# Four convolution layers on one core: smaller input batches in layer 0, and layer 1's chunks placed among layer 2's

## The chip, the core and the metric

The kernel runs on one core of a Trainium2 chip. The time is the device time of one execution in microseconds; before the change it is 16901.53 us, the median of three runs (16893.86 to 16957.51). The profile is one execution of 16909.8 us. PE is the tensor engine, PEld its weight loads, DVE the vector engine, ACT the scalar engine, POOL is GpSimd and SP the sync engine, of which the last two only issue transfers here.

## The reference

x is a batch of 32 images of 8 channels and 256 x 256 pixels. Four layers follow one another, each of the form x + f(gn(x)), where gn normalises each of four groups of two channels of an image:

```python
x = x + L0(gn(x))   # cellular automaton, learned automaton and a gate between them
x = x + L1(gn(x))   # 3x3 convolution of values quantised to -127..127, one scale for all images
x = x + L2(gn(x))   # 3x3 convolution
x = x + L3(gn(x))   # 5x5 mean of each channel
```

Layer 0 computes, from its normalised input (called drive where it is the automaton's):

```python
grid = drive
for _ in range(15):
    mapped = 3.9 * grid * (1 - grid)
    local = conv3x3(mapped, K_local, one kernel per channel)
    grid = 0.85 * (0.7 * mapped + 0.3 * local) + 0.15 * drive
cml = clip(grid, 0.0001, 0.9999)
nca = sigmoid(conv1x1(relu(conv3x3(x, Wp, bp)), Wu, bu))     # 8 -> 128 -> 8 channels
g = sigmoid(conv1x1(relu(conv3x3([x, cml, nca], Wg1, bg1)), Wg2, bg2))
out = g * cml + (1 - g) * nca
```

Because layer 1's scale needs the largest value of all 32 normalised images, layer 0 has to end for all images before layer 1 begins. So the kernel has two stages.

## The kernel before

**Stage one, layer 0.** Two streams of work are interleaved by hand; the order in which the program issues instructions is the order of each engine. The first stream is `lattice(b)`, the 15 steps of the automaton of image b. Each step has two halves of three channels: products with the neighbourhood (L391 from `state`, L393 from `rings`, the edge values that SyncE's transfers bring together), an addition on VectorE (L402), a square on ScalarE (L419) and the next transfer of `rings` (L259). Two more channels are done on VectorE alone, by nine taps a step (L338). The second stream is `gated()`, which computes the learned automaton and the gate of image b-1. After every piece, `lattice` says how many microseconds of other work should follow it, and the main loop takes that much from `gated()`. `errands` and `store` issue the transfers that bring images in and put the normalised ones into DRAM (`xn_d` with a border, `nr_d`, `xr_d`, `cr_d`), one at each half step.

`gated()` walks over n, a pair of row indices in each of the 16 blocks of an image; an image has 8 such n, and there are 256 in all. The input of the 3x3 convolution lies in tiles `im`: 24 x 3 partitions hold 8 channels at three horizontal and three vertical offsets, so that one product of 72 rows (L633) makes 512 pixels of 128 hidden channels. ScalarE takes each product through relu into `hh` (L638). A batch is four such products; during the next batch `second()` multiplies the four by `wu_sb` (L609), and when an n is complete `close` applies the sigmoid into `nh` (L587) and issues the edges `above` and `below` of it for the gate (L480). After each batch `pieces` runs the next piece of every gate that is due: first its loads `xq`, `cq`, edges and `xc` (L516, L480, L521), two batches later three products with `xq`, then with `cq`, then with `nh` (L530), then the edges (L538), the second convolution (L547), and at last the blend on VectorE and the store to `x1_d` (L560 to L568).

The `im` tiles are filled by `load(n, half)`: six transfers on GpSimd's queue (L504), one for each vertical offset and row index, each of 24 rows of 8248 bytes, for half of an n, which are 8 products. There are two buffers. When the eight products of one half are issued, the loads of the same half of n+1 are put among the first four products of the following half.

**Stage two, layers 1 to 3.** Three images are under way at once. A turn b of the loop (L864) issues layer 3 of image b-3, then layer 2 of image b-1, then layer 1 of image b. `among(work, tasks)` issues one piece of a layer's products and then the small tasks that are hung on that piece. Layers 1 and 2 have eight chunks of 512 columns; a chunk is four products (L726 three times, L730 once for the rows beside the block) in a PSUM tile of a pool of five. Layer 2's chunk is float32 and is taken out by VectorE (L771), layer 1's is bf16 and is taken out by ScalarE (L755) and added to by VectorE (L756); both then have their statistics counted (L772, L757). Layer 3 has four groups of ten products (L812 and L825), taken out by L832.

The rows beside a block come by `beside` (L143) on SyncE's queue: `xb` from `xh`, `qb` from `qh`, two transfers each. Statistics are computed by `stats_parts` in small steps, which go back and forth between VectorE, TensorE (L104, L111) and ScalarE, and by `by_group`, which brings the four groups' values to all partitions (L131 on VectorE, L133 on TensorE). In the code before, layer 1's statistics and its normalisation for layer 2 (`normal2`, L761), and the quantisation of the next image (`quantize1`, L742 to L706), are hung on layer 3's pieces. Layer 3's normalisation (`normal3`, L793) is hung on layer 2's chunks, and the statistics of layer 2's output are hung on layer 1's chunks. Layer 2's output goes to DRAM (L777) and comes back in another layout (`load3`, L786).

Of the kernel before, what the change touches and what calls it, by code (L numbers as in the profile page):

```python
# [9 lines left out]
F32 = mybir.dt.float32  # L10
# [7 lines left out]
P = 128  # L18
# [3 lines left out]
RB = H // HB  # L22
# [44 lines left out]
def kernel(  # L67
# [70 lines left out]
    def beside(queue, t, src, q):  # L138


        row, long = HB * WP, (HB - 1) * WP - 2
        for i, (p, to, at) in enumerate(((P - C, 1, 0), (0, 0, 1))):
            queue.dma_start(  # L143
                t[q + 24 * i : q + 24 * i + 24, :, :].rearrange("p k w -> p (k w)")[
                    :, to * WP : to * WP + long
                ],
                window(src, p * row + at * WP, [[row, C], [1, 3], [1, long]]),
            )
# [18 lines left out]

    with ExitStack() as es:
        wt = es.enter_context(tc.tile_pool(name="wt0", bufs=1))
        imp = es.enter_context(tc.tile_pool(name="im", bufs=2))  # L170
        qp = es.enter_context(tc.tile_pool(name="quarters", bufs=2))
        hp = es.enter_context(tc.tile_pool(name="h", bufs=3))
        ps_c = es.enter_context(tc.tile_pool(name="ps_c", bufs=3, space=PSUM))
# [313 lines left out]
        def gated():  # L487
# [1 line left out]

            run = 8 * WP - 2
            SLOTS = [k % 8 for k in range(HB)]
            due = {}
            ims, sums, halos = [], {}, {}

            def load(n, half):
                b, r2 = divmod(n, NCH)
                im = imp.tile([72, 2, 8 * WP], F32, name="im")
                ims.append(im)  # L500
                for dy in range(3):
                    for k in range(2):
                        at = ((2 * r2 + k) * RB + 8 * half + dy) * WP
                        nc.gpsimd.dma_start(  # L504
                            im[24 * dy : 24 * dy + 24, k, 0:run],
                            window(xn_d[b % 3], at, [[HP * WP, C], [1, 3], [1, run]]),
                        )
                        yield
# [87 lines left out]
            def pieces(batch):  # L596
                for g in due.pop(batch, ()):
                    w = next(g, None)
                    if w is not None:
                        due.setdefault(batch + 1, []).append(g)  # L600
                        yield w
# [3 lines left out]
            def second():  # L605
                n, pn, four = late.pop()
                for hh, r in four:
                    i, q = divmod(r, 4)
                    nc.tensor.matmul(  # L609
                        pn[32 * q : 32 * q + 32, :], wu_sb[:, i, :], hh,  # L610
                        start=i == 0, stop=i == 3,
                    )
                if four[-1][1] == RB - 1:
                    close(n, pn)

            batch, quarter = 0, None
            for half in range(2):
                for _ in load(0, half):
                    pass
            coming = iter(())  # L620
            for n in range(B * NCH):
                place[0] = n
                if n % 2 == 0:
                    quarter = {}

                due.setdefault(batch + 5, []).append(gate(n, quarter))
                for half in range(2):
                    im = ims.pop(0)
                    for rows in ((0, 1, 2, 3), (4, 5, 6, 7)):
                        four = []  # L630
                        for i, j in enumerate(rows):
                            ph = psum.tile([P, 512], F32, name="ph", tag="ps")
                            nc.tensor.matmul(  # L633
                                ph.rearrange("p (k w) -> p k w", w=W), wp_sb,
                                im[:, :, j * WP : j * WP + W], start=True, stop=True,
                            )
                            hh = hp.tile([P, 512], F32, name="hh", bufs=6)
                            nc.scalar.activation(hh, ph, AF.Relu, bias=bp_sb)  # L638
                            four.append((hh, 8 * half + j))
                            next(coming, None)  # L640
                            if i % 2 == 0:
                                next(coming, None)
                            if i == 1 and late:
                                second()
                                yield 1.05
                            yield 0.87
                        if half == 0 and rows[0] == 0:
                            pn = ps_n.tile([P, 512], F32, name="pn")
                        late.append((n, pn, four))
                        yield from pieces(batch)  # L650
                        batch += 1
                    coming = load(n + 1, half) if n + 1 < B * NCH else iter(())
            second()
            yield 1.05
            while due:
# [24 lines left out]
    with ExitStack() as es:  # L680
# [59 lines left out]
        def quantize1(b, x1, k):  # L740
            t = two.tile([P, 1024], F32, name="tq")
            nc.vector.tensor_scalar(  # L742
                t, x1[:, bass.ts(k, 1024)], stat1[:, b, 0:1], stat1[:, b, 1:2],
                ALU.subtract, ALU.mult,
            )
            quantize(
                qh[:, 4 * k : 4 * k + 4, 1 : 1 + W],
                t.rearrange("p (r w) -> p r w", w=W), sc[:, 0:1],
            )
# [17 lines left out]
        def layer2(b, x2, bn):  # L767
            for i in range(NCH):
                ps = conv3(xh, xb2, w2_sb, i)
                c = x2[:, bass.ts(i, 512)]  # L770
                nc.vector.scalar_tensor_tensor(c, ps, b2_sb, c, ALU.add, ALU.add)  # L771
                nc.vector.bn_stats(bn[:, i, :], c)  # L772
                yield
            x3 = x3_d[b % 2]
            for r in range(RB):
                m = r % 4 * 4 + r // 4
                nc.gpsimd.dma_start(  # L777
                    window(x3, r * W, [[H * W, C], [RB * W, HB], [1, W]]),
                    x2[C * m : C * m + C, :].rearrange("p (k w) -> p k w", w=W),
                )  # L780
# [64 lines left out]
        def among(work, tasks):  # L845
            for i in range(8):
                next(work, None)
                for task in tasks.get(i, ()):
                    task()
            for _ in work:  # L850
                pass
# [4 lines left out]
        def begin(bn):  # L856
            st = small.tile([P, 2], F32, name="st")
            parts = stats_parts(psum, bn, st, gavr_sb, "ps")
            next(parts)
            return st, parts  # L860

        with tc.manual_schedule():
            x1s[0] = load1(0)
            for b in range(B + 3):  # L864
                if b + 1 < B:
                    x1s[b + 1] = load1(b + 1)
                tasks = {i: [] for i in range(8)}
                if 1 <= b <= B:
                    st, parts = sums.pop(1)
                    for i in range(4):  # L870
                        tasks[i].append(step(parts))
                    tasks[3].append(lambda: normal2(x2s[b - 1], st))
                if b < B:
                    for k, i in enumerate((0, 1, 2, 4)):
                        tasks[i].append(lambda k=k: quantize1(b, x1s[b], k))
                    tasks[5].append(lambda: beside(nc.sync, qb, qh, 0))
                among(layer3(b - 3, ys.pop(b - 3)) if b >= 3 else iter(()), tasks)
                tasks = {}
                if 2 <= b <= B + 1:
                    for g in range(4):  # L880
                        tasks[g] = [lambda g=g: normal3(ys[b - 2], gss[b - 2], g)]
                    tasks[3].append(beside3)
                bn2 = small.tile([P, NCH, 6], F32, name="bn")
                among(layer2(b - 1, x2s[b - 1], bn2) if 1 <= b <= B else iter(()), tasks)
                tasks = {}
                if 1 <= b <= B:
                    st3, parts3 = begin(bn2)
                    for i in range(4):
                        tasks[i + 1] = [step(parts3)]

                    def groups():
                        gss[b - 1] = by_group(psum, st3)

                    tasks[6] = [groups]
                    ys[b - 1] = load3(b - 1)
                bn1 = small.tile([P, NCH, 6], F32, name="bn")
                if b < B:
                    x2s[b] = two.tile([P, NPX], F32, name="x2")
                among(layer1(b, x1s[b], x2s[b], bn1) if b < B else iter(()), tasks)
                if b < B:  # L900
                    sums[1] = begin(bn1)


def laid_out(inputs):
# [133 lines left out]
```

## Time and profile before

| stretch | from, us | to, us | what runs |
|---|---|---|---|
| first automaton | 0 | 387 | `lattice` of image 0 alone |
| stage one | 387 | 13768 | `lattice` of image b with `gated` of image b-1 |
| last gate | 13768 | 14025 | `gated` of image 31 alone |
| stage two | 14025 | 16910 | layers 1 to 3 in turns of 85.4 us |

The borders are the first and last starts of L633 and L393. Engines over the whole span: PE 15762.1 us busy, DVE 11707.7, ACT 5744.5, POOL 3820.6. The largest groups are L338 on DVE (3840 instructions of 1284 ns) and L633 on PE (8192 records, 4218.6 us busy; a float32 product stands as two records). L504 on POOL has 3072 instructions of 565 ns mean, 193.3 KB each, with a median of 9.0 us from issue to landing. In a line of the profile's waits, the first part is who waited, the second for whom, then the total, the number of waits and the longest. In a timeline line, the two numbers are start and duration, and the bracket has the idle time ahead of it and what ended it. In a line of stretches there follow, after the busy times and counts of the five engines in the order PE, PEld, DVE, ACT, POOL, the granted clock of TensorE, the share of DMA time and GB/s.

### The profile page before, as it was taken

The numbers are of one execution on the slowest core, as the hardware profiler recorded it, in microseconds if no ns is written. First come the engines' busy times: TensorE is split into PE (matmuls) and PEld (weight loads), VectorE is DVE, ScalarE is ACT, GpSimd is POOL, SyncE is SP. The second block draws the span as 40 slices with busy tenths as digits, with TensorE's granted clock in tenths as the row PEclk, the third lists the DMA queues.
The fourth block names the chain that finished last, engine by engine and source line by source line (L and its number), as shares of the span: only waits on it lengthen the run. The fifth ranks groups of instructions, "written<-read, shape, count | busy, mean of one in ns | idle before, by whom it ended". The sixth has DMA issues, their size and how long they took to land. (4 is left out here: it accounts for less than half of the span.)

```text
span 16909.8 us, 135970 instructions
## 1 busy us (share of the span) xinstructions
PE 15762.1 (93%) x42888; PEld 6291.4 (37%) x42888; DVE 11707.7 (69%) x14652; ACT 5744.5 (34%) x8862; POOL 3820.6 (23%) x6419
## 2 busy tenths in 40 slices
PE   5999999999999999999999999999999997999999
PEld 2333333333333333333333333333333332333333
DVE  7777777777777777777777777777777754555554
ACT  2333333333333333333333333333333342111110
POOL 1222222222222222222222222222222222111111
PEclk7999999999999999999999999999999998999999
DMA  4766666666677667676666666666666664555554
GB/s 102 148 140 140 137 145 139 140 140 139 143 144 144 143 142 144 144 145 137 141 143 145 140 140 144 139 137 140 142 145 141 142 125 103 113 111 111 114 114 97
DMA packets 861099, 2275.88 MB, mean 135 GB/s; under 512 B 296860, under 2 KB 500628, under 8 KB 780388
## 3 DMA queue, kind: packets, MB, share of 16 engines
q0 software_dynamic: 507904, 1492.90, 41.6%
q1 hardware_dynamic: 352484, 774.29, 23.0%
q8 instruction: 350, 5.73, 0.2%
q14 instruction: 361, 2.96, 0.1%
HBM read 1078.63 MB, written 471.38 MB: 92 GB/s over the span
## 5 line engine op out<-in xcount | busy, mean ns | idle before, releaser
L338 DVE SCALAR_TENSOR_TENSOR acc<-strip,taps_sb,acc 128x1024 f32<-128x1024 f32 x3840 | 4930.3, 1284 | 122.4 <-DMA strip<-strip 2.4
L633 PE MATMUL ph<-im,wp_sb 72*128 72x512 f32 x8192 | 4218.6, 632 | 492.8 <-ACT hh L638 248.2
L638 ACT ACTIVATE hh<-ph,bp_sb 128x512 f32<-128x512 f32 x4096 | 2764.0, 691 | 4873.6 <-PE ph L633 4818.6
L402 DVE SCALAR_TENSOR_TENSOR psc<-psc,flat 128x512 f32<-128x512 f32 x2880 | 1935.6, 696 | 3256.2 <-PE psc L393 3236.6
L391 PE MATMUL psc<-state,patch_sb 128*128 128x512 f32 x5760 | 2844.8, 632 | 74.5 <-ACT state L419 63.7
L393 PE MATMUL psc<-rings,ring_sb 80*128 80x512 f32 x5760 | 2727.2, 610 | 176.4 <-DMA rings<-state 176.0
L504 POOL DMA_DIRECT2D im<-xn_d x3072 | 1721.9, 565 | 3909.3 <-PE ph L633 3394.7
L633 PEld LDWEIGHTS ph<-im,wp_sb 72*128 72x128 f32 x8192 | 1522.0, 197 | 2694.9 <-issue 1887.0
L419 ACT ACTIVATE state<-psc,minus 128x512 f32<-128x512 f32 x2688 | 1690.9, 691 | 1816.3 <-DVE psc L402 1750.7
L391 PEld LDWEIGHTS psc<-state,patch_sb 128*128 128x128 f32 x5760 | 1131.5, 202 | 1730.3 <-issue 1411.0
L393 PEld LDWEIGHTS psc<-rings,ring_sb 80*128 80x128 f32 x5760 | 1112.4, 194 | 1636.6 <-issue 1592.5
L812 PE MATMUL psv<-xr,w_sb 128*128 128x512 f32 x2560 | 1200.6, 619 | 1.3 <-DVE xr L793 1.3
L609 PE MATMUL pn<-hh,wu_sb 128*32 128x512 f32 x8192 | 1172.8, 629 | 2.4 <-ACT hh L638 2.3
L568 POOL DMA_DIRECT2D x_d<-xc x256 | 149.9, 586 | 3896.8 <-DVE xc L563 3670.5
L777 POOL DMA_DIRECT2D x_d<-x x512 | 304.2, 610 | 2115.5 <-DVE x L771 1854.0
L530 PE MATMUL pg<-xq,wg_sb 128*128 128x512 f32 x1536 | 759.0, 633 | 0.0
L755 ACT ACTIVATE x<-psv,b_sb,sc 128x512 f32<-128x512 f32 x256 | 199.8, 780 | 1598.2 <-PE psv L730 1592.7
L812 PEld LDWEIGHTS psv<-xr,w_sb 128*128 128x128 f32 x2560 | 489.9, 197 | 660.4 <-issue 656.2
L726 PE MATMUL psv<-xh,w_sb 128*128 128x512 f32 x1536 | 708.0, 597 | 19.4 <-DVE xh L761 9.8
L530 PE MATMUL pg<-cq,wg_sb 128*128 128x512 f32 x1536 | 717.6, 603 | 0.0
L480 POOL DMA_DIRECT2D below<-nh x288 | 197.3, 685 | 1860.5 <-ACT nh L587 1860.5
L338 DVE SCALAR_TENSOR_TENSOR acc<-strip,taps_sb,d 128x1024 f32<-128x1024 f32 x480 | 613.0, 1277 | 0.0
(163 smaller groups left out, 12238.2 us busy)
## 6 DMA issues: line engine op xcount, KB each, us to landing
im<-xn_d POOLq DMA_DIRECT2D x3072, 193.3 KB, 9.0
rings<-state SPq DMA_DIRECT2D x1920, 159.5 KB
rings<-state SPq DMA_DIRECT2D x1920, 106.3 KB
strip<-strip SPq DMA_DIRECT2D x960, 126.0 KB
xn_d<-xb POOLq DMA_DIRECT2D x128, 516.0 KB, 11.9
nr_d<-xb POOLq DMA_DIRECT2D x128, 516.0 KB, 10.0
xq<-nr_d POOLq DMA_DIRECT2D x128, 516.0 KB, 5.2
cq<-cr_d POOLq DMA_DIRECT2D x128, 516.0 KB, 7.7
```

Source lines behind the costliest of these rows:

```text
L338: nc.vector.scalar_tensor_tensor(acc, strip[:, dy : dy + RQ, dx : dx + W], taps_sb[:, 3 * dy + dx : 3 * dy + dx + 1], d2 if dy == 1 and dx ...
L391: nc.tensor.matmul(pss[-1], patch_sb[:, c, :], inner(c), start=True, stop=False)
L393: nc.tensor.matmul(pss[c % HALF], ring_sb[:, c, :], rings[half][:, c % HALF, 0 : TX * SY].rearrange("p (x y) -> p x y", y=SY)[:, :, 0:TY], ...
L402: nc.vector.scalar_tensor_tensor(ps, ps, FLOOR, dr[:, c], ALU.max, ALU.add)
L419: nc.scalar.activation(inner(c), pss[c % HALF], AF.Square, bias=minus)
L504: nc.gpsimd.dma_start(im[24 * dy : 24 * dy + 24, k, 0:run], window(xn_d[b % 3], at, [[HP * WP, C], [1, 3], [1, run]]),)
L530: nc.tensor.matmul(o, wg1_sb[:, s, dx, :], src[:, :, dx : dx + W], start=s == dx == 0, stop=False,)
L609: nc.tensor.matmul(pn[32 * q : 32 * q + 32, :], wu_sb[:, i, :], hh, start=i == 0, stop=i == 3,)
L633: nc.tensor.matmul(ph.rearrange("p (k w) -> p k w", w=W), wp_sb, im[:, :, j * WP : j * WP + W], start=True, stop=True,)
L638: nc.scalar.activation(hh, ph, AF.Relu, bias=bp_sb)
L726: nc.tensor.matmul(o, w[:, dx, :], src[:, 2 * i : 2 * i + 2, dx : dx + W], start=dx == 0, stop=False,)
L812: nc.tensor.matmul(pss[k].rearrange("p (c w) -> p c w", w=W), w3_sb[:, dx, :], xr[:, k, mine, dx : dx + W], start=dx == 0, stop=stop,)
```

## The change

Two parts, independent of each other.

In `gated()`, `load(n, four)` now fills a tile for four products, a quarter of an n, and there are four buffers. A load again has six transfers, of half the bytes. They are issued among the first two products of the batch that follows, for the same quarter of n+1. The point is that data be asked for three batches ahead of its use. The order of the products and of everything else in the stream stays.

In stage two, layer 1 of image b and layer 2 of image b-1 are issued together, a chunk of layer 2 and then one of layer 1, so that VectorE has a longer stretch of TensorE work to keep up with. Layer 3's statistics can't be hung on layer 1 any longer; they move to layer 3's pieces of the next turn, next to those of layer 1's output. The fourth quantisation and the transfer of `qb` move up by one piece.

```diff
-        imp = es.enter_context(tc.tile_pool(name="im", bufs=2))
+        imp = es.enter_context(tc.tile_pool(name="im", bufs=4))
...
-            run = 8 * WP - 2
+            run = 4 * WP - 2
...
-            def load(n, half):
+            def load(n, four):
+
                 b, r2 = divmod(n, NCH)
-                im = imp.tile([72, 2, 8 * WP], F32, name="im")
+                im = imp.tile([72, 2, 4 * WP], F32, name="im")
                 ims.append(im)
                 for dy in range(3):
                     for k in range(2):
-                        at = ((2 * r2 + k) * RB + 8 * half + dy) * WP
+                        at = ((2 * r2 + k) * RB + 4 * four + dy) * WP
...
-                for half in range(2):
+                for i in range(4):
                     im = ims.pop(0)
-                    for rows in ((0, 1, 2, 3), (4, 5, 6, 7)):
-                        four = []
-                        for i, j in enumerate(rows):
...
-                            next(coming, None)
-                            if i % 2 == 0:
-                                next(coming, None)
-                            if i == 1 and late:
-                                second()
-                                yield 1.05
-                            yield 0.87
...
+                    four = []
+                    for j in range(4):
...
+                        for _ in range(3):
                             next(coming, None)
+                        if j == 1 and late:
+                            second()
+                            yield 1.05
+                        yield 0.87
...
-                    coming = load(n + 1, half) if n + 1 < B * NCH else iter(())
+                    coming = load(n + 1, i) if n + 1 < B * NCH else iter(())
...
                 tasks = {i: [] for i in range(8)}
+                if 2 <= b <= B + 1:
+                    st3, parts3 = sums.pop(2)
+                    for i in range(4):
+                        tasks[i].append(step(parts3))
+
+                    def groups():
+                        gss[b - 2] = by_group(psum, st3)
+
+                    tasks[5].append(groups)
...
-                    for k, i in enumerate((0, 1, 2, 4)):
-                        tasks[i].append(lambda k=k: quantize1(b, x1s[b], k))
-                    tasks[5].append(lambda: beside(nc.sync, qb, qh, 0))
+                    for k in range(4):
+                        tasks[k].append(lambda k=k: quantize1(b, x1s[b], k))
+                    tasks[4].append(lambda: beside(nc.sync, qb, qh, 0))
...
-                among(layer2(b - 1, x2s[b - 1], bn2) if 1 <= b <= B else iter(()), tasks)
...
+                ones_ = layer1(b, x1s[b], x2s[b], bns[0]) if b < B else iter(())
+
+                def both():
+                    for _ in layer2(b - 1, x2s[b - 1], bns[1]) if 1 <= b <= B else range(8):
+                        next(ones_, None)
+                        yield
+
+                among(both(), tasks)
+                if 1 <= b <= B:
+                    sums[2] = begin(bns[1])
+                    ys[b - 1] = load3(b - 1)
                 if b < B:
-                    sums[1] = begin(bn1)
+                    sums[1] = begin(bns[0])
```

More of the change, by code (lines that the diff above doesn't have):

```diff
@@ L616, in gated @@
             batch, quarter = 0, None
-            for half in range(2):
-                for _ in load(0, half):
+            for i in range(4):
+                for _ in load(0, i):
                     pass
@@ L626, in gated @@
                 due.setdefault(batch + 5, []).append(gate(n, quarter))
-                for half in range(2):
+                for i in range(4):
                     im = ims.pop(0)
-                    for rows in ((0, 1, 2, 3), (4, 5, 6, 7)):
-                        four = []
-                        for i, j in enumerate(rows):
[L632 to L639, printed above, removed]
-                            next(coming, None)
-                            if i % 2 == 0:
-                                next(coming, None)
-                            if i == 1 and late:
-                                second()
-                                yield 1.05
-                            yield 0.87
[L647 to L651, printed above, removed]
-                    coming = load(n + 1, half) if n + 1 < B * NCH else iter(())
@@ new lines, in gated @@
+                    four = []
+                    for j in range(4):
+                        ph = psum.tile([P, 512], F32, name="ph", tag="ps")
+                        nc.tensor.matmul(
+                            ph.rearrange("p (k w) -> p k w", w=W), wp_sb,
+                            im[:, :, j * WP : j * WP + W], start=True, stop=True,
+                        )
+                        hh = hp.tile([P, 512], F32, name="hh", bufs=6)
+                        nc.scalar.activation(hh, ph, AF.Relu, bias=bp_sb)
+                        four.append((hh, 4 * i + j))
+                        for _ in range(3):
+                            next(coming, None)
+                        if j == 1 and late:
+                            second()
+                            yield 1.05
+                        yield 0.87
@@ L653, in gated @@
+                    if i == 0:
+                        pn = ps_n.tile([P, 512], F32, name="pn")
+                    late.append((n, pn, four))
+                    yield from pieces(batch)
+                    batch += 1
+                    coming = load(n + 1, i) if n + 1 < B * NCH else iter(())
             second()
@@ L867 @@
                 tasks = {i: [] for i in range(8)}
+                if 2 <= b <= B + 1:
+                    st3, parts3 = sums.pop(2)
+                    for i in range(4):
+                        tasks[i].append(step(parts3))
+                    def groups():
+                        gss[b - 2] = by_group(psum, st3)
+                    tasks[5].append(groups)
                 if 1 <= b <= B:
@@ L882 @@
                     tasks[3].append(beside3)
-                bn2 = small.tile([P, NCH, 6], F32, name="bn")
-                among(layer2(b - 1, x2s[b - 1], bn2) if 1 <= b <= B else iter(()), tasks)
[L885 to L896, printed above, removed]
+                bns = [small.tile([P, NCH, 6], F32, name="bn") for _ in range(2)]
                 if b < B:
                     x2s[b] = two.tile([P, NPX], F32, name="x2")
-                among(layer1(b, x1s[b], x2s[b], bn1) if b < B else iter(()), tasks)
+                ones_ = layer1(b, x1s[b], x2s[b], bns[0]) if b < B else iter(())
[7 more added lines that the diff above has]
+                    ys[b - 1] = load3(b - 1)
                 if b < B:
-                    sums[1] = begin(bn1)
+                    sums[1] = begin(bns[0])
 def laid_out(inputs):
```

## The prediction

> **What bounds the kernel now.** I read the busy table first, then the stretches, then the waits of the tensor engine, then its timeline at the two places that the change touches.
>
> ```profile
> PE 15762.1 (93%) x42888; PEld 6291.4 (37%) x42888; DVE 11707.7 (69%) x14652; ACT 5744.5 (34%) x8862; POOL 3820.6 (23%) x6419
> ```
> ```profile
> 6000.00:8000.00 2000.00, 1901.70 (x5297) 755.16 (x5296) 1472.50 (x1713) 785.19 (x1226) 503.86 (x854) 0.95 0.70 144
> ...
> 15000.00:16000.00 1000.00, 924.66 (x2368) 382.99 (x2367) 546.84 (x1017) 128.04 (x168) 143.84 (x228) 0.94 0.51 114
> ```
> TensorE is busy for 95% of layer 0 and 92% of layers 1 to 3 (first pair of numbers after the span), at a granted clock of 0.95 and 0.94 (third from the end); VectorE has slack in both. So the end is set by TensorE's work, its gaps, and its slow clock. Its waits:
> ```profile
> PE ph L633 <- ACT hh L638: 248.2, 120, 4.9
> PE psc L393 <- DMA rings<-state: 176.0, 68, 18.4
> PE ph L633 <- DMA im<-xn_d: 126.2, 21, 7.6
> PE ps L133 <- DVE sel L131: 121.9, 32, 4.2
> PE ps L111 <- DVE t L108: 68.5, 36, 2.4
> ...
> PE ph L633 <- DMA above<-nh: 47.1, 8, 7.1
> ```
> Row 3 is the wait that part 1 of the change aims at. Its last row, and one more of 13.3 us put down to `xr_d<-xb`, are the same wait under other names: L633 reads nothing but `im` and weights, and all 31 stand at the same phase of an image. Together 186.7 us, 6.0 each. Rows 4 and 5 are the statistics between layer 2 and layer 3, which stand among layer 1's chunks.
>
> What a gap costs beyond itself shows in the timeline:
> ```profile
> 5370.30 1.02 PE L547 MATMUL pq<-g,wg_sb 128*128 128x512 f32 x2
> 5376.77 3.75 PE L633 MATMUL ph<-im,wp_sb 72*128 72x512 f32 x4 [5.45 <-DMA im<-xn_d]
> 5380.45 1.94 PE L609 MATMUL pn<-hh,wu_sb 128*32 128x512 f32 x8
> ...
> 5388.94 2.74 PE L393 MATMUL psc<-rings,ring_sb 80*128 80x512 f32 x6
> ```
> After the gap four products take 3.75 us, where 1.88 is usual: half the clock. The trace's clock records hold only 1.0 and 0.5. I set isolated gaps against them: of 21 gaps up to 1.25 us none is followed by half clock, of 4 near 1.5 us one, of 7 near 2 us six, of the longer ones all. After the 31 `im` waits the clock is halved for 304.9 us in all, so half of that, 152 us, is lost on top.
>
> Layer 1 in one period of layers 1 to 3:
> ```profile
> 15017.72 0.38 PE L730 MATMUL psv<-qb,w_bf 72*128 72x512 bf16 x1
> 15020.13 0.38 PE L111 MATMUL ps<-t,gavr_sb 128*128 128x1 f32 x2 [2.04 <-DVE t L108]
> ...
> 15021.49 1.49 PE L726 MATMUL psv<-qh,w_bf 128*128 128x512 bf16 x3
> ...
> 15029.47 0.59 PE L133 MATMUL ps<-sel,ones 128*128 128x8 f32 x2 [3.78 <-DVE sel L131]
> ...
> 15031.57 5.12 PE L812 MATMUL psv<-xr,w_sb 128*128 128x512 f32 x8
> ```
> A chunk of layer 1 (four bf16 products) takes 0.87 us at full clock and 1.70 after a gap; VectorE needs 1.33 for it (L756 and L757). So VectorE falls behind, each statistic waits behind its queue, TensorE waits for the statistic, and then layer 1 and the start of layer 3 (5.12 us for 3.5) run at half clock.
>
> [...] For the edge rows `xb` (24 rows from 8 partitions) [...] the trace shows 8 packets at a time of 2.40 us, 48 in all, so 14.7 us. [...]
>
> **Part 1: input in four buffers of 4 rows.** The order of TensorE, ScalarE and VectorE stays as it was; the space is the same (four halves for two wholes); the bytes are the same. Added: 3072 issues on GpSimd of 0.565 us, 1736 us; GpSimd is busy for 23%, would be for 33%, and nobody computes on it. Packets of 8248 B become two of 4120: unhindered (the trace's tenth percentile) they take 315 and 160 ns, so there is no more DMA work. Moved: a load was issued in the first four products of the next half and needed about 1.3 batches later (a batch of four products is some 13 us); now it has 3 batches, about 39 us. At the wait shown, the loads were issued from 5351 to 5361 and landed at 5376, in a stretch with the DMA engines full (share 1.02), for a need at 5371. With 39 us none of these should wait. Queued behind the extra issues on GpSimd are the gate's quarters `xq`, `cq` and edges; six issues delay them by 3.4 us. At the tight place `xq` was issued at 5343.9 and landed by 5353 at the latest, and its reader L530 came at 5362.6, so that holds by about 5 us.
> The most that this gives is 186.7 + 152 = 339 us. Some of it comes back as waits for `rings`, which then come due 11 us earlier in full DMA engines. At the place shown `rings` had landed by 5381, and without the wait would be needed at about 5379 and 5391: little or nothing. I keep 70%: **240 us**. Ends: 0 and 340.
>
> **Part 2: layer 1's chunks among layer 2's, layer 3's statistics one phase later.** The period now is 85.4 us (median distance of L761). TensorE's work in it at full clock: layer 2, 8 x 3.43 = 27.4; layer 1, 8 x 0.87 = 7.0; layer 3, 4 x 9.77 = 39.1; five statistics 1.3; sum 74.8. The other 10.6 are 6.1 of gaps (2.04, 3.78, 0.24) and some 4.5 lost to half clock.
> Paired chunks: TensorE 3.43 + 0.87 = 4.30, VectorE 1.39 + 1.33 = 2.7, with a normalisation of layer 3 (L793 twice, 0.99) 3.7: it keeps up, and the five PSUM buffers need not hold more than two pairs. So the gaps inside layer 1 go: **removed, 10.6**.
> Statistics in layer 3: L104 and L111 have over 3 us of products ahead of them, as layer 1's own had there already (no gap in the trace): nothing. L133 stands right after the last product of a group, whose eviction L832 (0.69) and two L131 (0.22 each) come before it on VectorE: **a gap of about 1.3 us**, by the table above too short to halve the clock.
> **The new wait: the edges.** Layer 1's first chunk now comes 3.43 + 0.65 us after layer 3, not 27 us later, and its `qb` rows are queued behind `xb` on the same engines. Counted from layer 3's start: L761 ended at 25.7 and `xb` was issued at 25.75; now full clock brings it 2 us earlier and the second set of small operations (5 x 0.19) and the like about 1.5 later, 25.3. From issue to release of the reader it is 16.7 us, or 18.2 where a load of x1 ran beside it:
> ```profile
> 14198.71 1.44 SPq L143 DMA_DIRECT2D xb<-xh  x2
> ...
> 14216.87 2.04 PE L730 MATMUL psv<-xb,w_sb 72*128 72x512 f32 x2 [13.79 <-DMA xb<-xh]
> ```
> So `xb` is there at 42.0 to 43.5, needed at 41.4 + 2.6 = 44.0: just in time. `qb` landed 3.5 us after `xb` in each period that I looked at: 45.5 to 47.0, needed at 41.4 + 3.43 + 0.65 = 45.5. Wait 0 to 1.5 us. New beside it: layer 2's result goes out some 17 us later against layer 3, so the loads of y and x1 run beside `xb`. In the one place of before where x1 did, `xb` was not slowed (12.5 us of packets), x1 was (12 for 6); for y I allow up to 3 us. I take 1.5 us of wait and 0.7 for the cases that halve the clock. Ends: 0, and 4.5 with 3 of slow clock.
> Sum for a period: 10.6 - 1.3 - 2.2 = 7.1; for 31, 220 us. The first two periods, whose statistics nothing covers, get 10 us worse: **210 us**. Ends: 280 and 50.
>
> **Sum:** 240 + 210 = 450; 16901.5 - 450 = **16450**.
>
> **The rivals.** A: the edges take the place of the statistics. For: `xb` and `qb` are within 2 us of their need, and a wait of 2 us brings the slow clock. Against: the fixed 14.7 us. Part 2 then gives 50: 16901.5 - 240 - 50 = 16610. B: part 1's gain is given back; the DMA engines are full in that stretch (1.02) whoever waits, so `rings` or `xq` take the wait over. Against: the mean share is 0.69, and 39 us reach past the full stretch. 16901.5 - 210 = 16690. C, slower than before: doubled issues make GpSimd late for quarters and edges in every one of the 256 row pairs, say 2 us and 2 of slow clock each, 1024 us in the worst case, a third of it 340, and the edges eat part 2: 16901.5 + 340 - 50 = 17190. For: GpSimd has at most eight transfers under way (L777 issues eight, then waits for the first). Against: 6 + 2.7 transfers a batch in 8 places allow 12 us each, and they take 9.
>
> **How the numbers follow.** Forecast 0.57, A 0.16, B 0.15, C 0.06, and 0.06 for A and B together, about 16850, which is no change. Time 16450. Range: from both parts at their best, 16901.5 - 340 - 280, about 16280, to past A and B, 16750. Faster 0.88, same 0.06, slower 0.06.
>
> **What would show it.** Right: no wait of L633 for `im`; L504 x6144; half clock in layer 0 down by some 300 us; period near 78; L133's gap 1.3; L730 waiting for `qb` by 1 to 2 us. Wrong: waits of L530 or L538 for `xq`, `cq` or edges; more waits for `rings`; L730 waiting 4 us or more.

## The result, and the profile after

The changed kernel takes 16325.74 us (median of 4 runs, 16309.52 to 16351.16), where the one before took 16915.62 in its runs beside it: a ratio of 0.965, with an interval of 0.9626 to 0.9674. That is about 590 us less, where 450 were forecast. The sum came out better than its parts: part 1 gave about twice its forecast, part 2 two thirds of it.

In the profile of the changed kernel, the lines that answer to those shown of before are first the busy times and the same two stretches:

```profile
PE 15452.2 (95%) x42888; PEld 6215.7 (38%) x42888; DVE 11705.9 (72%) x14652; ACT 5726.7 (35%) x8862; POOL 5598.2 (34%) x9491
```
```profile
6000.00:8000.00 2000.00, 1924.74 (x5406) 768.24 (x5404) 1502.97 (x1761) 797.86 (x1247) 763.12 (x1313) 0.96 0.67 145
15000.00:16000.00 1000.00, 938.81 (x2475) 393.49 (x2473) 574.05 (x1055) 130.50 (x171) 162.66 (x238) 0.97 0.52 117
```
TensorE has the same 42888 records, yet 310 us less busy time, because more of it runs at full clock (0.96 and 0.97 for 0.95 and 0.94). GpSimd is busy for 34% instead of 23%, with 3072 issues more. Then TensorE's waits:

```profile
PE ph L633 <- ACT hh L638: 251.3, 122, 4.9
PE psc L393 <- DMA rings<-state: 129.8, 37, 18.9
PE psv L729 <- DMA qb<-qh: 121.3, 30, 13.5
...
PE ps L133 <- DVE sel L131: 45.6, 32, 13.0
...
PE ps L111 <- DVE t L108: 3.6, 5, 1.0
```
No wait of L633 for a transfer is left, neither under the name of `im` nor under the two others. The waits for `rings` are fewer, 37 for 68. L133 and L111 have given up most of theirs. A new row stands third: L729 (L730 of the kernel before) waits for `qb`, the edge rows of layer 1; of its 30 waits the kernel before had only the one of 13.5 us.

One period in the timeline of TensorE, from the end of layer 3 to layer 1's first chunk, and then the transfers of the edge rows in SyncE's queue:

```profile
15115.73 1.98 PE L811 MATMUL psv<-xr,w_sb 128*128 128x512 f32 x4
15118.76 0.39 PE L133 MATMUL ps<-sel,ones 128*128 128x8 f32 x2 [1.05 <-DVE sel L131]
...
15131.43 1.02 PE L729 MATMUL psv<-xb,w_sb 72*128 72x512 f32 x2
15132.29 0.81 PE L725 MATMUL psv<-qh,w_bf 128*128 128x512 bf16 x3
15137.67 0.39 PE L729 MATMUL psv<-qb,w_bf 72*128 72x512 bf16 x1 [4.57 <-DMA qb<-qh]
```
```profile
15112.86 1.43 SPq L143 DMA_DIRECT2D xb<-xh  x2
15116.65 5.37 SPq L143 DMA_DIRECT2D qb<-qh  x2
```
`xb`, issued first, is there when its product comes (no bracket at 15131.43); `qb`, behind it in the queue, is 4.57 us late.

Where the time went, by the kernels' own marks (L633 is layer 0's first and last product):

| stretch | before, us | after, us | difference |
|---|---|---|---|
| start to first L633 | 386.7 | 380.9 | -6 |
| first to last L633 | 13638.6 | 13184.8 | -454 |
| last L633 to the end | 2884.5 | 2750.9 | -134 |

For layer 0 I set TensorE's gaps and the clock records of the two traces side by side. The columns of half clock give the time at half clock outside gaps, of which half is lost (a record of L633 takes 592 ns in the median at full clock and 1061 at half, in the trace of before); each piece is put down to the longest gap near it.

| layer 0 | gaps before | half clock before | gaps after | half clock after |
|---|---|---|---|---|
| wait for `im` (all names) | 186.7 us in 31 | 321 us | 0 | 0 |
| wait for `rings` | 139.8 in 60 | 462 | 100.8 in 32 | 288 |
| all gaps | 665.2 | 1207 | 443.9 | 758 |

All in all 221 us of gaps and 449 / 2 = 224 of slow clock, 445 of the 454. `im` has 187 + 160 = 347 of it, `rings` 39 + 87 = 126; the rest went the other way by 28.

### The profile page after: what moved, and what is told of

It is laid out like the page before. It is cut to its first block, busy times and chain, and to the rows that moved or that the text cites. A ratio compares the mean times of both kernels' runs of the same rounds, so it can differ in the third digit from the quotient of the medians.

```text
span 16316.6 us, 141125 instructions
## 1 busy us (share of the span) xinstructions
PE 15452.2 (95%) x42888; PEld 6215.7 (38%) x42888; DVE 11705.9 (72%) x14652; ACT 5726.7 (35%) x8862; POOL 5598.2 (34%) x9491
## 4 chain that ended last, share of the span: by engine, by line
PE 74%; DVE 13%; DMA 7%; ACT 3%; issue 2%; SPq 1%; POOL 0%; DVEq 0%; ACTq 0%; POOLq 0%
PE ph L633 17%; PE psc L391 14%; PE psc L393 13%; PE pg L531 9%; DVE acc L338 7%; PE psv L725 5%; PE pn L610 5%; PE psv L811 4%; DMA qb<-qh 3%; DMA rings<-state 2%; PE psv L729 2%; PE pq L548 1%; PE pg L543 1%; PE pg L539 1%; DVE psc L402 1%
## 5 line engine op out<-in xcount | busy, mean ns | idle before, releaser
L505 POOL DMA_DIRECT2D im<-xn_d x6144 | 3458.3, 566 | 3250.0 <-PE ph L633 1434.7
L633 PE MATMUL ph<-im,wp_sb 72*128 72x512 f32 x8192 | 4091.7, 615 | 308.8 <-ACT hh L638 251.3
L391 PE MATMUL psc<-state,patch_sb 128*128 128x512 f32 x5760 | 2812.0, 626 | 74.1 <-ACT state L419 63.3
L393 PE MATMUL psc<-rings,ring_sb 80*128 80x512 f32 x5760 | 2713.5, 607 | 129.8 <-DMA rings<-state 129.8
L633 PEld LDWEIGHTS ph<-im,wp_sb 72*128 72x128 f32 x8192 | 1489.5, 193 | 2425.4 <-issue 1587.8
L811 PE MATMUL psv<-xr,w_sb 128*128 128x512 f32 x2560 | 1162.9, 600 | 1.3 <-DVE xr L792 1.3
L610 PE MATMUL pn<-hh,wu_sb 128*32 128x512 f32 x8192 | 1133.9, 609 | 3.3 <-ACT hh L638 3.3
L725 PE MATMUL psv<-xh,w_sb 128*128 128x512 f32 x1536 | 753.0, 629 | 9.6 <-issue 9.6
L531 PE MATMUL pg<-xq,wg_sb 128*128 128x512 f32 x1536 | 749.3, 626 | 0.0
L531 PE MATMUL pg<-cq,wg_sb 128*128 128x512 f32 x1536 | 713.7, 601 | 0.0
L831 DVE TENSOR_TENSOR y<-psv,y 128x512 f32<-128x512 f32 x256 | 177.1, 692 | 593.7 <-PE psv L811 593.7
```

Of the source, the lines that this page charges most:

```text
L391: nc.tensor.matmul(pss[-1], patch_sb[:, c, :], inner(c), start=True, stop=False)
L393: nc.tensor.matmul(pss[c % HALF], ring_sb[:, c, :], rings[half][:, c % HALF, 0 : TX * SY].rearrange("p (x y) -> p x y", y=SY)[:, :, 0:TY], ...
L505: nc.gpsimd.dma_start(im[24 * dy : 24 * dy + 24, k, 0:run], window(xn_d[b % 3], at, [[HP * WP, C], [1, 3], [1, run]]),)
L531: nc.tensor.matmul(o, wg1_sb[:, s, dx, :], src[:, :, dx : dx + W], start=s == dx == 0, stop=False,)
L610: nc.tensor.matmul(pn[32 * q : 32 * q + 32, :], wu_sb[:, i, :], hh, start=i == 0, stop=i == 3,)
L633: nc.tensor.matmul(ph.rearrange("p (k w) -> p k w", w=W), wp_sb, im[:, :, j * WP : j * WP + W], start=True, stop=True,)
```

## The experiments

The theory to test: part 1 works by the lead of the loads (how long before its use a tile is asked for), and part 2's new wait is `qb`'s place behind `xb`. In some of these kernels the lines stand up to three further down.

**Each part alone.** For the first, the loop of layers 1 to 3 is that of before; for the second, layer 0 is.

> Part 1 alone, layers 1 to 3 as before. In the trace of the changed kernel the stretch from the first to the last L633 is 13185 us, where it was 13639, so 454 of the 593 us are put down to part 1. If the two parts are independent, this one is at 16450 us (0.973 of before) with the same stretch of 13185 within 20 us. Rival: the parts work on each other (through the clock or through what is in the DMA queues at the border), then it lies more than 60 us from that.

> Part 2 alone, layer 0 as before. By the traces it gives 134 us of the 593: 16780 us (0.992), period of layers 1 to 3 at 81.7 us with a wait of L729 for qb of 3.6 us in each. Rival: as for part 1 alone, more than 60 us away.

Part 1 alone: 16433.96 us, 0.9721 (0.9703 to 0.9738), layer 0 in 13147.3 us. Part 2 alone: 16766.92 us, 0.9917 (0.9897 to 0.9937), rest in 2750.0 us, period 81.8. The losses of 0.0279 and 0.0083 sum to 0.0362 against 0.035 for both: the parts are independent, and layer 0 has some three quarters of the gain. With part 2 alone the `im` wait is there in full (32 gaps, 191 us), under two names mainly:

```profile
PE psc L393 <- DMA rings<-state: 178.4, 71, 17.9
PE psv L730 <- DMA qb<-qh: 121.5, 30, 13.5
PE ph L633 <- DMA im<-xn_d: 86.5, 14, 7.5
PE ph L633 <- DMA above<-nh: 85.8, 15, 7.3
```

**Small transfers without the long lead.** Each load is held back by one batch, so its lead is the one of before, or by two (`> 2` in place of `> 1`).

```diff
-            coming = iter(())
+            coming, held = iter(()), []
...
-                    coming = load(n + 1, i) if n + 1 < B * NCH else iter(())
+                    if n + 1 < B * NCH:
+                        held.append((n + 1, i))
+                    ready = held and (len(held) > 1 or n + 1 == B * NCH)
+                    coming = load(*held.pop(0)) if ready else iter(())
```

> The changed kernel, but each load of im is held back by one batch, so that it is issued in the second batch before its use, as in the kernel before, while the transfers are still of half the bytes. Theory of the lead: the wait for im came from loads asked for too late in a stretch of full DMA engines; it comes back in most images, perhaps shorter because each need is for half the bytes: 10 to 31 waits, 60 to 190 us, with the slow clock 100 to 340 us over the changed kernel, 16425 to 16665 us. Rival, the size: smaller transfers that are spread evenly are what cured it; then there are no waits for im and the time is that of the changed kernel, 16326 within 50 us. The waits for rings tell the same: if they fell because the transfers are small, they stay near 130 us, if because of the lead, they go back towards 176.

> The same, held back by two batches, so that a load is issued in the batch just before its use. Theory of the lead: waits for im in every image and several to an image, over 300 us in all, and a time above the kernel before's layer 0, so over 16600 us in all. Rival, the size: still near 16330 us.

With two batches: 16491.91 us, 0.9758 (0.9737 to 0.978), layer 0 in 13341.8 us. With one: 18339.11 us in a single run, layer 0 in 15192.9. The waits of the first, then of the second:

```profile
PE psc L393 <- DMA rings<-state: 111.0, 36, 18.7
PE ph L633 <- DMA im<-xn_d: 78.4, 24, 7.0
```
```profile
PE ph L633 <- DMA im<-xn_d: 1427.5, 257, 17.0
```
Neither theory was right alone. With the lead of before the `im` waits come back, as the theory of the lead had it, 25 of them, but at 3.3 us each instead of 6.0: layer 0 is 297 us shorter than before and some 157 longer than in the changed kernel. So about two thirds of part 1 come from the halved transfers, one third from the longer lead. The lead itself was not longer than before where the waits stand: in the median the last of a tile's six transfers was issued 7.4 us before its need, where it was 10.5 in the kernel before, but the tile was complete 9.7 us after that issue and not 16.5. And the waits for `rings` stay low with the short lead, so it was the size, not the lead, that cured them. Their place in an image says the same: before, 25 of them stood between 293 and 313 us after an image's start (its first L633), each with four to six transfers of `im` under way, and there is none of these in the changed kernel, in part 1 alone, or with the lead of two batches. With the halved transfers the bytes are also spread evenly over the batches here; the next run takes that away again, though at the longer lead. Rows of 8248 B last 715 ns in the mean and rows of 4120 B 303, while those of `rings` last 575 and 570: a row of `rings` is not moved faster, but it has to stand behind less. That last step is argued from these means and not shown by a run.

**The same bytes per batch as before.** The loads of two quarters together, twelve transfers in every other batch.

```diff
-                    coming = load(n + 1, i) if n + 1 < B * NCH else iter(())
+                    due2 = i % 2 == 1 and n + 1 < B * NCH
+                    coming = chain(load(n + 1, i - 1), load(n + 1, i)) if due2 else iter(())
```

> The changed kernel, but the loads of two quarters are issued together, twelve transfers in one batch of every two: the bytes asked for in each batch are then those of the kernel before, in transfers of half the size, with leads of two and three batches. Waits for rings were 138.5 us in 59 in the stretch of layer 0 before and 101 in 32 after. If it is the bursts that delayed rings, they go back to some 139, with the slow clock 60 to 120 us over the changed kernel, 16390 to 16450 us. If it is the size of a transfer, or how many bytes eight of them have under way, they stay at 80 to 110 us; then at most a few waits for im come back, and the time is 16330 to 16390 us.

16206.32 us, 0.9587 (0.9562 to 0.9613): 120 us faster than the changed kernel, where I expected no gain at all. Layer 0 takes 13058.6 us. `im` waits are back, 15 of 1.4 us, but those for `rings` fell further, and most of them under the 1.25 us up to which no isolated gap of before was followed by half clock:

```profile
PE psc L394 <- DMA rings<-state: 70.3, 33, 19.0
```
Bursts of these smaller transfers did not delay `rings` here: 70.3 us of waits, where the changed kernel has 129.8. What is left of these waits stands at 34 to 40 us after an image's start in every kernel but the one with a lead of one batch, where stores of the normalised image, the first `rings` and the loads meet; their median fell from 2.9 us to 1.1, and the half clock after them from 288 us to 68. Why they are shorter here stays open. The loads do begin earlier: the DMA engines are busy for 0.93 between 10 and 15 us after an image's start, where it is 0.52 in the changed kernel (means over 30 images). But the crowd is not over earlier, with 0.95 between 36 and 40 us for 0.72; and in the kernel before the engines are at 0.96 and 1.00 in these two stretches, and its waits there have a median of 2.9 us too.

**Four times the issues.** Tiles of two rows in eight buffers.

> The changed kernel with tiles of two rows in eight buffers: the same bytes, four times the issues of before (12288, 6940 us of GpSimd by 0.565 each), lead of three and a half batches. The forecast costed the issues at nothing because GpSimd does nothing else. If that holds at twice the number too, the time is 16326 within 50 us, with no wait for im. Rival, the cost of issues: GpSimd at over half busy and eight transfers under way at most make quarters and edges late; waits of L531 or L539 for them, 100 us or more in all, 16430 us or more.

16277.99 us, 0.9632 (0.9615 to 0.9649). GpSimd is busy for 8216 of the 12800 us between 400 and 13200. TensorE never waits for `im`, and for `rings` only 5.0 us in layer 0 after the first image, but the rival is there too:

```profile
PE pg L531 <- DMA xq<-nr_d: 162.5, 30, 10.3
```
The quarters behind the issues come late, once an image. So the cost that the forecast put at nothing is nothing at twice the issues of before, where L531 waits for no transfer, and no longer at four times; it is about as large as what the still smaller transfers give, for the time cannot be told from the changed kernel's (0.9626 to 0.9674).

**Who delays qb.** First its transfers on GpSimd's queue (`beside(nc.gpsimd, qb, qh, 0)`), then the load of x1 among the paired chunks.

> The changed kernel with the two transfers of qb issued on GpSimd's queue instead of SyncE's, so that they don't stand behind those of xb. Theory: the wait of L729 for qb (3.6 us a period and the slow clock after it) comes from the order in SyncE's queue and goes; the period falls from 81.7 to 76 to 77 us, the time by 140 to 170 us, to 16155 to 16185 us (0.956 of before). Rival: the eight DMA engines that serve the edge rows are full with xb, y and x1 whatever the queue; then qb lands as late as now and the time stays at 16326 within 40 us. A second rival: xb, 1 us ahead of its need now, is pushed behind its need by qb, and a wait for xb of 1 to 3 us takes its place; 16220 to 16290 us.

> The changed kernel with the load of the next x1 (2 MB) issued among the paired chunks instead of at the start of a turn, so that it no longer runs beside xb and qb. In the kernel before qb ended 3.5 us after xb, in the changed one 6.0. If the load of x1 is what stretches it, it goes back to 3.5 to 4.5 us, the wait for qb falls from 3.6 to 1 to 2 us, mostly too short for the slow clock, and the time to 16210 to 16260 us. If it is the stores of out or the load of y, qb stays at 5.5 us or more after xb and the time within 40 us of 16326.

`qb` on GpSimd's queue: 16532.91 us, 0.978 (0.976 to 0.9801), which is 207 us slower than the changed kernel, with a period of 88.0 us. None of the three expectations. Its transfers stand behind those of y and x1 there, 4 MB that are still being moved: `qb` ends 8.9 us after `xb`, not 6.0, and both waits are there:

```profile
PE psv L729 <- DMA qb<-qh: 239.8, 31, 12.0
...
PE psv L729 <- DMA xb<-xh: 75.9, 30, 13.4
```
The second kernel was to move x1's load and did not: GpSimd's queue has nothing to wait for there, so the load is issued some 4 to 6 us after L760 in both kernels. Its 16301.29 us (0.9645, 0.9627 to 0.9663) say nothing on x1, and period and wait are unchanged. What it does show is how far layer 0 varies from run to run: the changed kernel and the six others with the same layer 0 have it at 13147 to 13209 us. Which of the loads of y and x1 and the stores of `out` stretches `qb` is not shown by any run.

**qb ahead of xb.** The fourth quantisation and `qb`'s transfers come before `normal2`.

```diff
-                    for k in range(4):
-                        tasks[k].append(lambda k=k: quantize1(b, x1s[b], k))
-                    tasks[4].append(lambda: beside(nc.sync, qb, qh, 0))
+                    for k, i in enumerate((0, 1, 2, 2)):
+                        tasks[i].append(lambda k=k: quantize1(b, x1s[b], k))
+                    tasks[2].append(lambda: beside(nc.sync, qb, qh, 0))
```

> The changed kernel with the fourth quantisation and the transfers of qb moved ahead of normal2 and the transfers of xb (both now hang on layer 3's third piece), all still on SyncE's queue. Theory of the order: qb waits for no more than its place behind xb, so it lands long before its need. xb's packets then end at about 20 us after L760 starts, with its reader's need at about 19 to 20, so a wait for xb of 0 to 2 us may take the place; the period falls from 81.7 to 76 to 79 us and the time by 90 to 170 us, to 16155 to 16240 us. Rival, capacity: y, x1, xb and qb together need the engines until then in any order, so the wait only changes its name; 16326 within 40 us.

16151.01 us, 0.9531 (0.9504 to 0.9558); last L633 to the end 2600.0 us, 151 less than in the changed kernel; the period is 76.0 us. In SyncE's queue and on TensorE:

```profile
15087.35 2.45 SPq L143 DMA_DIRECT2D qb<-qh  x2
15093.66 3.84 SPq L143 DMA_DIRECT2D xb<-xh  x2
```
```profile
15113.23 1.10 PE L729 MATMUL psv<-xb,w_sb 72*128 72x512 f32 x2 [0.81 <-DMA xb<-xh]
15114.16 0.81 PE L725 MATMUL psv<-qh,w_bf 128*128 128x512 bf16 x3
15114.81 0.38 PE L729 MATMUL psv<-qb,w_bf 72*128 72x512 bf16 x1
```
No wait for `qb` is left, that for `xb` is 0.8 us in the period shown, and between 13820 and 15900 us the clock is never halved. The place of `qb` behind `xb` was the cause, and capacity was not: the same bytes are moved in a period that is 5.7 us shorter. The edit also issues `qb` earlier, now 6.3 us ahead of `xb` instead of 3.8 behind it; that part is not separated from the order.

**Both sides of the edges at once.** One side on SyncE, the other on ScalarE.

```diff
-            queue.dma_start(
+            (queue, nc.scalar)[i].dma_start(
```

> The changed kernel with one side of each of xb and qb issued by SyncE and the other by ScalarE, so that both sides are under way together. If what makes an xb packet last 2.4 us is that eight engines read from the same eight partitions (48 packets of 15472 B in 14.7 us are 50 GB/s for one side after the other, and qb's 371 KB in 6.3 us of the kernel before are 59), two sides at once read from twice as many, xb ends after 8 to 10 us instead of 14.7, qb with it, no wait for edges is left and the time is 16326 - 165 = 16160 within 40 us. If the eight DMA engines themselves are the limit, xb still takes 14 to 15 us and the time stays at 16326 within 40 us.

16280.86 us, 0.9599 (0.956 to 0.9637), period 79.5 us: between the two, and by its time alone not clear of the changed kernel. In three of the 30 periods that the trace has both sides ran together and `xb`'s packets took 8.6 to 8.9 us, 742 KB at 85 GB/s; in the others the second side began 2.1 to 9.0 us after the first, and they took 10.4 to 17.3. So the 50 GB/s of one side after the other (742 KB in 14.7 us) is no limit of the edge rows' transfers as such. Whether the eight packets at a time of one queue and those of the other are moved by the same engines the trace does not tell, and that it is the partitions read that make a packet last 2.40 us on one queue is not shown by any run. Why the second side began late is open: both are issued within 0.1 us of each other in the period that I looked at.

**L133, and all together.** The groups' values one piece later (`tasks[6]` for `tasks[5]`) on top of `qb` ahead of `xb`, and then with the loads by two.

> The changed kernel with qb ahead of xb, and L131 and L133 (the groups' values) moved from layer 3's sixth piece to its seventh, where four products stand between the last eviction and L133. Theory: L133's gap of 1.05 us is the wait for L832's counterpart and for L131 alone, and goes; the period falls from 76.0 to 75.0 us, the time by 30 us to about 16120. Rival: xb, which was just in time, is now needed 1 us earlier and takes the wait over; the period stays at 76.

> The same with the loads of im issued for two quarters at a time, in one batch of every two. If the gains add up: 16326 - 175 (order of the edges) - 120 (loads by two) - 30 (L133) = 16000 us, 0.945 of before, with waits for rings near 70 us and a period of 75 us. If the gain of the loads by two hung on chance in the placing of the transfers, layer 0 goes back to the changed kernel's and the time is near 16120.

One piece later: 16125.56 us, 0.9526 (0.9499 to 0.9553), period 75.9: no change that the intervals can tell. L133's gap is gone, and the rival is right on where it went:

```profile
PE psv L729 <- DMA xb<-xh: 61.6, 25, 15.8
```
`xb` waits now in 25 products instead of 6, 61.6 us for 28.1: what TensorE saves ahead of the 15 us of `xb`'s packets, it waits behind them.

All together: 16073.62 us, 0.95 (0.9475 to 0.9524), the lowest median here, though its interval overlaps that of the kernel without the loads by two. That is 74 us short of the sum of the gains. Layer 0 takes 13092.7 us and keeps most of the gain of the loads by two; `xb` waits for 54.0 us.

## Why the prediction was right, and where its sums were off

The causes named for both parts and their direction were right, and the time lay in the range, near its lower end. That it lay in the range was in part luck: part 1 gave more than the 340 us put as its upper end, and had part 2 given its 210, the time would have been below 16280.

**Part 1, what is removed.** Waits and slow clock of `im` were to give at most 339 us; they gave 347, with no such wait left. (Not all 31 waits stood at one phase: 29 lay between 197 and 229 us after an image's start, the two others in the first and the last image.) A tile is now asked for 34 us ahead in the median, not 39, and that is enough. The step "some of it comes back as waits for `rings`", which took off 30%, had the wrong sign: `rings` gave 126 us more. I had looked at one image's place beside the wait for `im`, and had not asked what the 60 waits for `rings` in layer 0 stood behind; 25 of them stood beside the big loads, 90 us later. That the bytes stay the same was right, that the size of a transfer therefore has no effect was not: halving it gave about 300 of the 454 us, by the run with the lead of two batches.

**Part 1, what is added.** 3072 issues at no cost: confirmed; no wait of L531 or L539 is to be seen, and GpSimd is at 34%, with at most eight transfers under way in both traces. A transfer of `im` lands in 6.6 us in the median, instead of 9.0. Rival C has its place at four times the issues.

**Part 2, the gaps in layer 1.** Removed as forecast: L111 keeps 3.6 us of 68.5. L133's gap was put at 1.3 us and too short for the slow clock; it is 1.05, and no half clock follows it.

**Part 2, the new wait.** This term was mis-sized, and so the period fell to 81.7 us and not to near 78. It was put at 1.5 us and 0.7 of slow clock, with ends of 0 and 4.5 with 3; in the periods from 13820 to 16100 us it is 3.7 us (103.7 in 28) and 116.1 / 28 / 2 = 2.1 of slow clock. 10.6 - 1.05 - 5.8 leaves 3.75, and the period fell by 3.7, from 85.4. The chain of times for `xb` held: 14.7 us of packets in the median and in time. For `qb` I took 3.5 us behind `xb` from periods in which no load of y or x1 was under way and added nothing for them, though I had seen that these come to lie beside it; I gave them only to `xb`. It took 6.0; that y and x1 are the reason is likely by what lies beside it, but no run shows it. So rival A was half true, and part 2 gave 134 us for 210.

The two errors had opposite signs and cancelled in part: 454 for 240 is 214 too little forecast, 134 for 210 is 76 too much, and 588 for 450 leaves 138.

## What to carry to other kernels

Price a gap of TensorE with the slow clock behind it, which here cost about as much as the gaps (224 us beside 221 of the gain in layer 0), and look for the short waits that can be brought under the length at which it sets in (here between 1.25 and 2 us). When a stage moves closer to its transfers, write down the order in their queue and what else is being moved at that time: the same two transfers in the other order, issued a little earlier, were worth 151 us of layers 1 to 3. The size of a transfer can be a cost to other queues even where the bytes stay the same: with halved transfers at the lead of before, the waits for `rings` came to 111.0 us and not 176.0.

## What was not expected of the hardware

Gaps as short as 2 us were enough to halve TensorE's clock: in the trace of before, isolated gaps up to 1.25 us never did (21 of them), those near 2 us did in six of seven, and the changed kernel agrees (1.05 never in 28). And a lead of one batch less, 13 us, can be worth 1850 us: from two batches to one, layer 0 went from 13341.8 to 15192.9 us, since then about every fourth tile came late (257 waits of 5.6 us for 1024 tiles), and the granted clock of the whole run was 0.90, where it was 0.956 with two batches.
